# A time-mix and feed-forward kernel: the next block's normalisation moved to ScalarE, and weight splits spread over the first block's chunks

## The chip, the cores and the metric

The kernel runs on one core of a Trainium2 chip. The metric is the device time of one execution in microseconds (us); shorter is better. Five engines work side by side, each through its own instructions in order: TensorE (PE in the profile; its weight loads are PEld), VectorE (DVE), ScalarE (ACT), GpSimd (POOL) and SyncE (SP), which here only issues DMAs. An instruction that waits for another engine holds up everything behind it on its own engine.

## The reference

The input x is 4 x 1024 x 512. The kernel computes x + A(LN(x)) + F(LN(x)), where LN is a layer norm over the 512 features:

```python
xx = concat([x[:, 1:2], x[:, :-1]], axis=1) - x
k = (x + xx * mix_k) @ Wk.T          # 704 hidden
r = (x + xx * mix_r) @ Wr.T
state = state * w + relu(k_t)         # scan over time
out = layernorm((state * r) @ Wv.T) * gamma + beta      # A
D = gelu(float16(x) @ W0.T + bias0)   # 2048 hidden
E = float16(D) @ W1.T + bias1         # F
```

## The kernel before, in words

The tokens are cut into eight blocks of 512. Everything between the engines' instructions is written out by hand: the loops run under a manual schedule, so the order of the calls is the order on each engine.

**A block's loop.** Each block runs `for n in range(NN)` with NN = 16; one turn is called **chunk n** here. A chunk takes 128 of the 2048 hidden units. `up(i, n)` (L862) is the first product of the feed-forward part, eight matmuls of 512 columns into a PSUM bank `pd`: four with the high terms of W0 (`xf`, `w0h`), four with the low terms (`w0l`). The Gelu (L876, tile `d`, ScalarE) and a widening copy (L879) follow. `down` (L888) is the second product, eight matmuls with the low and then the high term of W1 (tile `w`). The up product runs two chunks ahead: in the first block, chunk n issues on TensorE up(n+2), then down(n), then a **piece** of the time-mix work, if the chunk has one. In the first block these are `raw_halves` (chunk 1), `three_pass` for r with h = 1 to 4 (chunks 3, 5, 7, 9; PSUM tiles `pa`, `pb`) and the output products `po` (chunks 12 to 15).

**Splits.** Weights and activations are split into terms so that fast matmuls keep the precision. `split` (L198) does it for W0 and W1: ScalarE writes the high term (L199), VectorE then the low one (L200). `split_kr` (begins L288) splits a tile of Wk or Wr: VectorE writes `wu` (L278) and `wd` (L285), ScalarE turns them into the first two terms `wt` (L294, L295), VectorE writes the third (L296); SyncE stores all three. `split_wv` (L308) does the same for Wv (`vu`, `vd`, `wv`); the half tile h = 5 takes two VectorE and four ScalarE instructions (L321, L322). All weights are split in the first block, a few at the start of the second, and reloaded later.

**What sets the order within a chunk.** First the followers of the chunk before (`after()` of a piece: ScalarE copies `a` out of `pa`, L707, VectorE makes `y`, L708, and so on), then the Gelu, then the jobs that `put(n, ...)` placed in `bg[n]`, in the order of the `put` calls, and last, in the first block, the split of W1 for chunk n+2: `waiting.append((d, load_w1(*nxt)))`. In the second block an odd chunk's Gelu comes after its jobs.

**PSUM.** `up`, the pieces and the output products take their banks in turn from one ring of four (`ps_mm`). A product can't start before the tile that had the bank four allocations earlier has been read by ScalarE or VectorE.

**The next block's x.** While the first block runs, the x of the second is loaded, its statistics are taken (`stats`, L354 and L355, VectorE), GpSimd makes 1/sqrt(var + eps) (`rstd_of`, L348 and L349), VectorE normalises (`norm_apply`, L358), then sixteen VectorE transposes (`turn`, L380) bring it into `xnT`. ScalarE makes the half-precision copy `x16` (L395) and the scaled copies (L403), VectorE mixes neighbouring tokens (L417, L421), ScalarE widens `x16` into `xf` (L442), which the second block's first up product reads.

Chunk by chunk, the first block's jobs that the change touches are: statistics in chunk 1, `norm_apply` in chunk 3, `first_kr(h)` (the split of Wr's tile h) in chunks 1, 3, 5, 7, transposes in chunks 4, 5, 7, 8, 9 (1, 4, 5, 1, 5 of them), `split_kr(1, 0, h)` for h = 2, 0, 1 in chunks 7, 10, 11, and `split_wv` for h = 0, 1, 2, 3, 5 in chunks 12, 13, 15, 15, 15; h = 4 follows in chunk 2 of the second block.

Of the kernel before, what the change touches and what calls it, by code (L numbers as in the profile page):

```python
# [14 lines left out]
AF = mybir.ActivationFunctionType  # L15
# [7 lines left out]
def time_mix_and_gelu_ffn(  # L23
# [32 lines left out]
    nc = tc.nc  # L56
# [4 lines left out]
    NS = TB // P  # L61
# [2 lines left out]
    Q = 32  # L64
    QS = 62
    RAW_OUT = 1
    WV_FIRST = {0: 12, 1: 13, 2: 15, 3: 15, 5: 15}
    S = 4096.0
    WS = 4096.0
    MASK = -4096  # L70
    OWN = dict(tag="q", bufs=QS)

    NF = HID // P
# [283 lines left out]
    def normalize(dst, src, mean, rstd):  # L357
        nc.vector.tensor_scalar(dst, src, mean, rstd, ALU.subtract, ALU.mult)  # L358

    norm = {}  # L360
# [9 lines left out]
    def norm_apply(i, xs):  # L370
        mv, rstd = norm.pop(i)
        for s in range(NS):
            normalize(xs[:, s, :], xs[:, s, :], mv[:, s, 0:1], rstd[:, s : s + 1])

    def transposed(xn, first=0, end=(P // Q) ** 2):
        src = xn.rearrange("p s (c i a) -> p s c i a", c=NC, a=Q)
# [531 lines left out]
    state = {}  # L908
# [53 lines left out]
    with tc.manual_schedule(engines=engines):  # L962
        for i in range(len(blocks)):
            j = i + 1
            tail = 4 if i == LAST else 0
            by_columns = range(NS // 2, NS) if tail else ()
            pieces, bg, early = defaultdict(list), defaultdict(list), defaultdict(list)

            def put(n, fn, *args, **home):
                bg[n].append(lambda: fn(*args, **home) if home else fn(*args))  # L970

            def first_kr(h):
                ks[0, 1, h] = split_kr(0, 1, h)
# [29 lines left out]
            if i == 0:  # L1003
                state["x"] = x_next
                piece(1, raw_halves, i)
                for h in range(1, NF):
                    piece(2 * h + 1, three_pass, i, 1, h)
                for c in range(NC):
                    put(2 + c - (c == 0), split_w0, 2, c)
                    put(c // 2, load_w0, 3, c)  # L1010
                    put(5 + c, split_w0, 3, c)
                put(1, stats, *range(NS))
                put(3, lambda: norm_apply(j, state["x"]))
                for c in range(NC):
                    put(c // 2, split_first_xr, c)
                for n, h in ((7, 2), (10, 0), (11, 1)):
                    put(n, split_kr, 1, 0, h, **OWN)
                for h in range(1, NF):
                    put(2 * h - 1, first_kr, h)
                put(4, turn, 0, 1)  # L1020
                put(5, turn, 1, 5)
                put(7, turn, 5, 10)
                put(8, turn, 10, 11)
                put(9, turn, 11, 16)
                put(9, load_late_constants)
                put(12, split_half)
                for g in range(NN // G):
                    put(11 + (g or NN // G), store_w0l, g)
                put(15, store_weights)
                mix_at = (11, 12, 13, 15)  # L1030
            else:
                order = [(0, h) for h in range(NF)] + [(1, h) for h in range(NF)]
                halves_ahead_of = (3 if i == LAST else NF, NF)
                for k, (kind, h) in enumerate(order):
                    for half in range(2):
                        if k == halves_ahead_of[half]:
                            piece(half_at[half], half_pass, i, half)
                    piece(full_at[k], three_pass, i, kind, h)
                    if (kind, h) not in made:
                        put({(0, 3): 1, (0, 4): 2, (1, 0): 4}[kind, h], fetch_kr, i, kind, h)  # L1040
                    elif k > 1:
                        put(full_at[k - 2], fetch_kr, i, kind, h)
                xr_at = {1: (2, 3, 4, 5), LAST: (1, 2, 2, 3)}.get(i, (2, 2, 3, 3))
                for c, n in enumerate(xr_at):
                    put(n, split_xr, i, c)
                if j <= LAST:
                    put(2, fetch_x)
                    for s in range(NS):
                        put(3 + s // 2 if i == 1 else 4, stats, s)
                    put(5, lambda: norm_apply(j, state["x"]))  # L1050
                    turns = (4, 4, 4, 4) if i == 1 else (4, 5, 4, 3)
                    for k in range(sum(turns)):
                        unit = next(n for n in range(4) if k < sum(turns[: n + 1]))
                        put(6 + unit, turn, k, k + 1)
                mix_at = (10, 12, 13, 14)
# [3 lines left out]
            if j <= LAST:  # L1059
                for c in range(NC):  # L1060
                    put((10, 10, 11, 12)[c], x16, j, c)
                for c, n in enumerate(mix_at):
                    early[n].append((j, c))
                    put(n, mixed, j, c)
                    put(n + (n == 10), split_xk, j, c)
                for h, n in {0: WV_FIRST, 1: {NF - 1: 2}}.get(i, {}).items():
                    put(n, split_wv, h)
                put(13, fetch_kr, j, 0, 0)
                put(14, fetch_kr, j, 0, 1)

            pe = [ps_e.tile([P, C], F32, tag="pe", name=f"pe_{i}_{s}") for s in range(NS)]
            for n in range(NN):
                ahead = n + AHEAD
                if ahead == NN and j <= LAST:
                    xf = next_xf
                nxt = (i, ahead) if ahead < NN else (j, ahead - NN)
                paired = i > 0 and n < NN - tail
                order = HIGH_FIRST if paired and n % 2 == 0 else LOW_FIRST
                end = lambda s: NN - tail if s in by_columns else NN
                products, gelu = up(*nxt) if nxt[0] <= LAST else (None, None)  # L1080

                def hidden(p):
                    if products:
                        products(p, order if paired else HIGH_FIRST)

                def outputs(p):
                    if n < NN - tail:
                        down(n, range(NS), *operands, p, order, end=end)

                if n < NN - tail:  # L1090
                    operands = waiting.pop(0)
                if not paired:
                    hidden(0)
                    hidden(1)
                elif n % 2 == 0:
                    hidden(0)
                else:
                    hidden(1)
                    outputs(1)
                    hidden(0)  # L1100
                works = [follow() for follow in followers]
                works = [w for w in works if next(w, works) is None]
                several(scaled_now, *early[n])
                if i == 0 or n == out_at[0] or (n > out_at[0] and i < RAW_OUT):
                    finished(*works)
                    works = []
                followers = []
                if behind_works:
                    waiting.append(behind_works.pop()())
                if gelu and not paired:  # L1110
                    d = gelu()
                if ahead + 1 == NN and j <= LAST:
                    next_xf = ffn_input(j)
                if not paired:
                    outputs(1)
                outputs(0)
                if gelu and i > 0:
                    w1 = load_w1(*nxt)
                    if not paired:
                        waiting.append((d, w1))  # L1120
                two_on = (i, ahead + 2) if ahead + 2 < NN else (j, ahead + 2 - NN)
                if two_on[0] <= LAST:
                    load_w0l(*two_on)
                jobs = [
                    lambda s=s: finish(i - 1, s, e16s[s])
                    for s in (2 * n, 2 * n + 1)
                    if s < len(e16s)
                ]
                for work, *args in pieces[n]:
                    followers.append(work(*args))  # L1130
                if i == 0 and ahead + 2 < NN:
                    load_w1_raw(ahead + 2)
                woven(works, jobs + bg[n])
                if i == 0:
                    waiting.append((d, load_w1(*nxt)))
                elif paired and n % 2 == 0:
                    hidden(1)
                    outputs(1)
                    behind_works.append(lambda gelu=gelu, w1=w1: (gelu(), w1))
                elif paired:  # L1140
                    waiting.append((gelu(), w1))
                store_weights()
# [66 lines left out]
```

## Time and profile before

| what | value |
|---|---|
| median of 3 runs | 858.14 us (857.48 to 858.91) |
| the profiled execution's own time | 857.93 us |
| its span | 856.1 us |
| TensorE | busy 847.0 us (99%), 3772 matmuls |
| VectorE | busy 687.1 us (80%), 1130 instructions |
| ScalarE | busy 438.1 us (51%), 748 instructions |
| GpSimd | busy 80.4 us (9%) |
| DMA | 166.72 MB, mean 195 GB/s |
| granted TensorE clock | 0.999 |

The first block lasts from the start to about 131 us, the second to about 234 us. A matmul is listed with the time that it takes to pass through, which overlaps its neighbours'; the distance from one start to the next is what it costs. For 512 columns that is 0.227 us, and 0.43 us for the unsplit products of the first block. In the timeline, equal instructions in a row are one line: start, time from first start to last end, engine, line, operation, tiles, count, and in square brackets the idle time before it with what ended it.

### The profile page before, as it was taken

What the parts mean: (1) busy time and instruction counts of PE and PEld (TensorE: products, weight loads), DVE (VectorE), ACT (ScalarE), POOL (GpSimd) and SP (SyncE); (2) the same over time, 40 slices, a digit from 0 to 9 for tenths busy, and PEclk for the clock granted to TensorE, in tenths of its full rate; (3) what the DMA queues carried; (4) which work ended last, traced back from release to release, by engine and by line L of the source; (5) the groups of instructions that cost most, each with busy time, mean ns of one, the idle gap of its engine ahead of it and who ended that gap; (6) DMA issues with size and microseconds to landing.
All of it is one profiled execution on the core that took longest, in us unless ns stands there. A gap on an engine that the chain in (4) does not pass through costs nothing.

```text
span 856.1 us, 11350 instructions
## 1 busy us (share of the span) xinstructions
PE 847.0 (99%) x3772; PEld 595.2 (70%) x3772; DVE 687.1 (80%) x1130; ACT 438.1 (51%) x748; POOL 80.4 (9%) x145
## 2 busy tenths in 40 slices
PE   9999999999999999999999999999999999999998
PEld 8556646667767767667777667677777667676776
DVE  6789898999868988789786897778796897876446
ACT  5857665546534563445725455344653545634422
POOL 1210000000211001000021001100011200200012
PEclk9999999999999999999999999999999999999999
DMA  9756995745467544856358455594465755467513
GB/s 279 252 178 239 306 282 193 249 151 182 148 230 225 172 136 149 288 165 209 130 170 284 148 180 172 159 308 146 151 193 161 272 173 181 127 220 247 169 54 111
DMA packets 120902, 166.72 MB, mean 195 GB/s; under 512 B 21487, under 2 KB 57740, under 8 KB 120844
## 3 DMA queue, kind: packets, MB, share of 16 engines
q1 hardware_dynamic: 120396, 165.34, 60.4%
q8 instruction: 30, 0.49, 0.2%
q10 hardware_dynamic: 448, 0.66, 0.2%
q14 instruction: 28, 0.23, 0.1%
HBM read 141.31 MB, written 24.64 MB: 194 GB/s over the span
## 4 chain that ended last, share of the span: by engine, by line
PE 82%; DVE 7%; DMA 5%; ACT 2%; issue 2%; SPq 2%; DVEq 0%; ACTq 0%
PE pd L862 22%; PE pe L888 22%; PE pa L695 14%; PE oa L792 7%; PE pb L446 7%; PE ob L800 4%; PE ph L724 3%; DMA x<-in_L_attn_x 2%; PE ob L802 1%; DMA krd<-wt 1%; DMA w0raw<-in_L_ffn_W 1%; SPq L239 1%; DVE w0l L200 1%; DVE wd L285 1%; ACT w L199 1%
## 5 line engine op out<-in xcount | busy, mean ns | idle before, releaser
L888 PE MATMUL pe<-w,d 128*128 128x512 f32 (+1 forms) x1008 | 262.9, 389 | 3.8 <-DVE w L200 3.4
L862 PE MATMUL pd<-xf,w0h 128*128 128x512 f32 x512 | 150.8, 415 | 0.1
L862 PE MATMUL pd<-x,w0l 128*128 128x512 f16 x512 | 132.2, 381 | 0.0
L876 ACT ACTIVATE d<-pd,late_sb 128x512 f16<-128x512 f32 x128 | 87.2, 681 | 75.4 <-PE pe L888 47.4
L862 PEld LDWEIGHTS pd<-xf,w0h 128*128 128x128 f32 x512 | 96.2, 188 | 28.4 <-issue 2.8
L888 PEld LDWEIGHTS pe<-w,d 128*128 128x128 f32 x504 | 94.7, 188 | 23.6 <-DVE e L835 1.2
L708 DVE SCALAR_TENSOR_TENSOR y<-pb,a 128x512 f32<-128x512 f32 x74 | 50.9, 688 | 65.5 <-PE pb L446 54.8
L888 PEld LDWEIGHTS <-d 128*128 128x128 f16 x524 | 50.6, 98 | 64.1 <-issue 5.1
L862 PEld LDWEIGHTS <-w0l 128*128 128x128 f16 x512 | 44.1, 98 | 62.2 <-issue 16.1
L879 ACT CAST d<-d 128x512 fp32r<-128x512 f16 x128 | 79.4, 620 | 10.3 <-PE pe L888 6.3
L380 DVE STREAM_TRANSPOSE xnT<-x 32x512 f32<-32x512 f32 x112 | 78.6, 702 | 2.2
L707 ACT ACTIVATE a<-pa 128x512 f32<-128x512 f32 x74 | 44.1, 596 | 70.2 <-PE pa L695 70.2
L348 POOL TENSOR_SCALAR ry<-mvy 128x1 f32<-128x1 f32 x32 | 18.9, 591 | 460.5 <-DVE mvy L355 460.5
L792 PE MATMUL oa<-wv,hg 128*128 128x512 f32 x140 | 54.5, 389 | 0.0
L792 PE MATMUL oa<-wv,lg 128*128 128x512 f32 x140 | 54.5, 389 | 0.0
L695 PE MATMUL pa<-lr,kr 128*128 128x512 f32 x136 | 52.9, 389 | 0.0
L695 PE MATMUL pa<-hr,kr 128*128 128x512 f32 x136 | 52.9, 389 | 0.0
L695 PE MATMUL pa<-hk,kr 128*128 128x512 f32 x132 | 51.4, 390 | 0.0
L695 PE MATMUL pa<-lk,kr 128*128 128x512 f32 x132 | 51.4, 389 | 0.0
L710 ACT ACTIVATE y<-y 128x512 f32<-128x512 f32 x35 | 22.1, 631 | 53.7 <-DVE y L708 53.7
L333 ACT CAST hg<-ug 128x512 fp32r<-128x512 f32 x35 | 21.7, 620 | 37.1 <-DVE ug L278 37.1
L807 DVE SCALAR_TENSOR_TENSOR oy<-ob,oa 128x512 f32<-128x512 f32 x28 | 19.3, 688 | 25.8 <-PE ob L802 25.8
(175 smaller groups left out, 1411.2 us busy)
## 6 DMA issues: line engine op xcount, KB each, us to landing
kr<-krd SPq DMA_DIRECT2D x201, 256.0 KB, 4.4
w<-w1d SPq DMA_DIRECT2D x112, 256.0 KB, 2.8
w<-w1d SPq DMA_DIRECT2D x112, 128.0 KB, 2.7
w0l<-w0d SPq DMA_DIRECT2D x108, 128.0 KB, 3.5
xres<-in_L_attn_x SPq DMA_DIRECT2D x32, 256.0 KB, 4.7
x<-in_L_attn_x SPq DMA_DIRECT2D x31, 256.0 KB, 5.0
krd<-wt SPq DMA_DIRECT2D x30, 256.0 KB, 3.3
out<-xres SPq DMA_DIRECT2D x28, 256.0 KB, 3.6
```

The costliest lines, as they stand in the source:

```text
L380: nc.vector.transpose(dst[i * Q : (i + 1) * Q, :, :, j, :], src[j * Q : (j + 1) * Q, :, :, i, :],)
L446: return nc.tensor.matmul(dst, w[:, c, :], src, start=(c == 0), stop=(c == NC - 1))
L695: nc.tensor.matmul(pa, w[p][:, c, :], xs[j, c][p], start=(c == 0 and p == 0), stop=(c == NC - 1 and p == 1),)
L707: nc.scalar.activation(a, pa, AF.Copy, scale=1.0 + 1.0 / S)
L708: nc.vector.scalar_tensor_tensor(y, pb, -1.0 / S, a, ALU.mult, ALU.add)
L724: nc.tensor.matmul(pa, w[:, c].rearrange("p two k -> p (two k)"), xs[j, c][p], start=(c == 0 and p == 0), stop=(c == NC - 1 and p == 1),)
L792: nc.tensor.matmul(pa, gs[i, h][p][:, cols], wv[h][p], start=(h == 0 and p == 0), stop=(h == NF - 1 and p == 1),)
L800: nc.tensor.matmul(pb, gs[i, h][2][:, cols], wv[h][2], start=(h == 0), stop=False)
L862: nc.tensor.matmul(pd, weights(c, p), src[c][p], start=(c == 0 and p == order[0]), stop=(c == NC - 1 and p == order[1]),)
L876: nc.scalar.activation(d16, pd, AF.Gelu, bias=b0_sb[:, n : n + 1], scale=1.0 / WS)
L879: nc.scalar.copy(d, d16)
L888: nc.tensor.matmul((sums or pe)[s], d[p][:, s * P : (s + 1) * P], w1[p][:, cols], start=(n == first and p == order[0]), stop=(n == end(s) ...
```

## The change

Six edits, all of them in what the first two blocks' chunks do:

1. The statistics of the second block's x move from chunk 1 to chunk 2.
2. Its normalisation leaves VectorE (one instruction for each of four tiles, chunk 3). ScalarE does it in two instructions a tile, one with the negated mean as bias and one with 1/std as scale, for two tiles in chunk 3 and two in chunk 4. GpSimd negates the means.
3. A new list, `behind_w1[n]`, is worked off after the chunk's split of W1. `first_kr`, `split_kr(1, 0, h)` and the ScalarE normalisation go there.
4. `split_kr(1, 0, 2)` moves from chunk 7 to chunk 4.
5. The transpose of chunk 4 joins those of chunk 5.
6. `split_wv` of the half tile h = 5 moves from chunk 15 of the first block to chunk 3 of the second, that of h = 4 from chunk 2 of the second to its chunk 6.

```diff
-    WV_FIRST = {0: 12, 1: 13, 2: 15, 3: 15, 5: 15}
+    WV_FIRST = {0: 12, 1: 13, 2: 15, 3: 15}
...
+    def norm_by_scalar(i, xs, tiles):
+        mv, rstd = norm[i]
+        if 0 in tiles:
+            nc.gpsimd.tensor_scalar_mul(mv[:, :, 0], mv[:, :, 0], -1.0)
+        for s in tiles:
+            for factors in ({"bias": mv[:, s, 0:1]}, {"scale": rstd[:, s : s + 1]}):
+                nc.scalar.activation(xs[:, s, :], xs[:, s, :], AF.Identity, **factors)
...
+            behind_w1 = defaultdict(list)
...
-                put(1, stats, *range(NS))
-                put(3, lambda: norm_apply(j, state["x"]))
+                put(2, stats, *range(NS))
+                behind_w1[3].append(lambda: norm_by_scalar(j, state["x"], range(2)))
+                behind_w1[4].append(lambda: norm_by_scalar(j, state["x"], range(2, NS)))
                 for c in range(NC):
                     put(c // 2, split_first_xr, c)
-                for n, h in ((7, 2), (10, 0), (11, 1)):
-                    put(n, split_kr, 1, 0, h, **OWN)
+                for n, h in ((4, 2), (10, 0), (11, 1)):
+                    behind_w1[n].append(lambda h=h: split_kr(1, 0, h, **OWN))
                 for h in range(1, NF):
-                    put(2 * h - 1, first_kr, h)
-                put(4, turn, 0, 1)
-                put(5, turn, 1, 5)
+                    behind_w1[2 * h - 1].append(lambda h=h: first_kr(h))
+                put(5, turn, 0, 5)
...
-                for h, n in {0: WV_FIRST, 1: {NF - 1: 2}}.get(i, {}).items():
+                for h, n in {0: WV_FIRST, 1: {NF: 3, NF - 1: 6}}.get(i, {}).items():
                     put(n, split_wv, h)
...
                     waiting.append((d, load_w1(*nxt)))
+                    for job in behind_w1[n]:
+                        job()
```

## The prediction

> **What bounds the kernel now.** I read the page first. Its chain of work that ended last is mostly TensorE, and the only sizeable wait in the groups of instructions is the second product's for VectorE's low term of W1:
>
> ```profile
> PE 82%; DVE 7%; DMA 5%; ACT 2%; issue 2%; SPq 2%; DVEq 0%; ACTq 0%
> L888 PE MATMUL pe<-w,d 128*128 128x512 f32 (+1 forms) x1008 | 262.9, 389 | 3.8 <-DVE w L200 3.4
> ```
>
> TensorE's timeline then says where: in the first block, at chunks 3, 5, 7 and 9.
>
> ```profile
> 52.16 1.95 PE L888 MATMUL pe<-w,d 128*128 128x512 f16 x8 [1.67 <-DVE w L200]
> 62.46 1.95 PE L888 MATMUL pe<-w,d 128*128 128x512 f16 x8 [0.26 <-DVE w L200]
> 73.05 1.94 PE L888 MATMUL pe<-w,d 128*128 128x512 f16 x8 [0.53 <-DVE w L200]
> 84.08 1.94 PE L888 MATMUL pe<-w,d 128*128 128x512 f16 x8 [0.99 <-DVE w L200]
> ```
>
> Between the starts of consecutive matmuls, less the usual 0.23, these four cost 1.81, 0.41, 0.68 and 1.14: 4.0 us. TensorE's other losses after 40 us come from the same starts: 1.3 us at 112 (the next block's `xf`), 1.3 at 132 (`e`, L835) and 0.7 at 154 (a bank that `a`, L707, must empty). From 156 us on it never waits. So what the change is worth is decided before 190 us, and any lateness of TensorE then stays to the end.
>
> **First block: statistics and W1 (edits 1 and 3).** Before, chunk 1 on VectorE goes: `w0l` (to 42.08), statistics 3.20, two splits of `xr` 3.77, `first_kr` 1.8 (three instructions 0.46, 0.72, 0.61 apart), then W1 of chunk 3, which lands at 52.10. Without statistics and `first_kr` ahead of it, that W1 starts at 42.08 + 3.77 = 45.85 and ends by 46.5; TensorE wants it at 50.35. The 1.81 goes; chunk 5's 0.41 goes too (its W1 by 57.4, wanted at 60.2). TensorE is then 2.2 us early. The statistics now start after chunk 2's half-tile work, at 52.4, and end at 55.6; W1 of chunk 4 follows at 55.6 to 56.2, wanted at 56.65: covered by 0.4 us.
>
> **ScalarE's normalisation (edits 2 and 4).** These rows price it:
>
> ```profile
> 57.52 1.91 DVE L358 TENSOR_SCALAR x<-x,mvx,rx 128x512 f32<-128x512 f32 x4
> 45.46 0.32 POOL L348 TENSOR_SCALAR rx<-mvx 128x4 f32<-128x4 f32 x1 [12.75 <-DVE mvx L355]
> 45.85 1.79 POOL L349 TENSOR_TENSOR rx<-rx,nhalf 128x4 f32<-128x4 f32 x1
> 168.20 1.04 POOL L349 TENSOR_TENSOR rx<-rx,nhalf 128x4 f32<-128x4 f32 x1
> 96.27 0.71 ACT L403 ACTIVATE xk<-xnT,rest_sb 128x512 f32<-128x512 f32 x1
> 96.89 0.71 ACT L403 ACTIVATE xr<-xnT,rest_sb 128x512 f32<-128x512 f32 x1
> 65.58 1.15 ACT L199 ACTIVATE w0h<-w0raw 128x512 fp32r<-128x512 f32 x2
> ```
>
> VectorE saves 1.83. The two-step form is not in the trace. Nearest is L403, which also takes a factor from a tile: 0.71 each, 0.62 apart; the second step needs the first, so 0.74 after it. Two tiles: 2.7 us, all four 5.4 (bounds: 8 x 0.48, the closest ScalarE spacing in this stage, = 3.9; 8 x 0.75 = 6.0). The negation on GpSimd is also unseen: 0.31, as its neighbour add (0.2 to 1.8).
>
> ScalarE reaches the normalisation at 54.0 and must wait. Statistics end 55.6, add and negation to 56.4, the power 1.79 more: 58.3. I take 1.79 and not 1.04 because it is the row of the same block, with VectorE busy beside it; the later five rows of 1.04 fall where VectorE waits for the result. With 1.04 all that follows is 0.8 earlier. [...]
>
> From 58.35, spaced as in the rows around 62 us, ScalarE issues: rest of two tiles 1.96, two `wt` 1.06, `a` 0.48, Gelu and cast 1.23, `w0h` 0.53, W1 0.53, two tiles 2.7, two `wt` of the split moved here from chunk 7 1.06, Gelu and cast 1.23, `w0h` 0.53 and the second `w0h`, 0.63. That is 11.95 us: the second `w0h` of chunk 5 is done at 70.3. Before it was done at 66.7. It is the last quarter of W0 for up(8), whose fourth matmul stood at 67.67 and, being 2.2 early, now wants it at 65.45. **So TensorE stalls 4.9 us in chunk 6 and is 2.7 late, where it had been 2.2 early.**
>
> [...]
>
> **To the end of the block (edits 3 and 5).** VectorE's transposes stand behind that `w0h`: `w0l` at 70.4, five transposes of 0.715 to 74.55, W1 of chunk 7 until 75.25, so TensorE starts at 75.3 against 73.05. Now `first_kr` follows W1, and the next chunk's `a` (L707) follows `first_kr` on ScalarE: `a` ends 2.2 after W1's term, the next piece wants its bank after 1.8. That adds 0.4: 2.7 late. The same in chunk 9: W1 at 86.4 (84.02), then 0.4: 2.8 late. W1 of chunks 10 to 12 is in time, the closest by 0.15.
>
> VectorE's own lateness grows: W1 of chunk 11 comes at 95.9 (91.06), that of 13 at 104.3 (102.19), and as the split of Wk's tile 1 now stands behind W1, chunk 14's at 113.6 (109.68). `xf` follows it on ScalarE: 115.9 against 112.00, so TensorE is 3.9 late. At 131 edit 6 takes 1.07 of VectorE ahead of `e` away; with TensorE later than VectorE by that, 1.1 of the 1.3 waited there comes back. **First block: 2.8 late.**
>
> SyncE issues the moved stores in the same new order: those of the tile-2 split stand ahead of W1's load for chunk 9, which is issued at about 69.5 instead of 66.27; ScalarE wants it at 81. Wv's loads go out at about 94.5 to 98 and are wanted from 102. I cost both at nothing; were the cover gone, they would cost 2 to 4 us.
>
> **Second block (edit 6).** VectorE, ScalarE and TensorE are all 2.8 late here, so I use the times of before and add that at the end. Without the tile-4 split in chunk 2, `a` runs at 152.0 and not 154.49, and TensorE's 0.7 at 154 goes. VectorE is 2.3 earlier: statistics 156.7 to 158.3. But then come the half tile's `vu` and `vd`, and its four ScalarE instructions stand in front of this Gelu:
>
> ```profile
> 158.12 0.68 ACT L876 ACTIVATE d<-pd,late_sb 128x512 f16<-128x512 f32 x1
> ```
>
> They run from 158.75 to 161.1 (they wait for `vd`, 159.45), so the Gelu ends at 161.8 instead of 158.8. It empties the bank that `three_pass` of k's tile 4 takes at 159.79: TensorE goes on 2.0 late. In chunk 6 the tile-4 split (1.8 on VectorE, behind transposes already 2.3 late) stands ahead of `a`, Gelu and `gh`. The Gelu of chunk 8 ends at 183.5 and the bank is wanted at 180.4: 3.15 late. The Gelu of chunk 9 ends at 187.5, wanted at 183.12: 4.4 late. **Second block: 4.4 late.** If the banks there have more room than I read, this is 0 or -0.7.
>
> **Sum.** 2.8 + 4.4 = 7.2 on the profiled execution's 857.93, which is 0.2 under the median of the runs: **865.0 us**.
>
> **Rivals.**
> - *It works as written*: W1's waits go and ScalarE's work hides. For it: ScalarE is busy only 51%, and idles 2.9 us before `wt` at 59.80. It decides where the second `w0h` is done by 65.45, 4.9 earlier than my sum. Price: -4.0, -0.7 at 154 and the 1.1 at `e`, 852 to 854 us. Chance 0.09.
> - *The moved Wv splits hide*: first block as above, second -0.7: 857.93 + 2.1 = 860.0. For it: VectorE still has 0.3 to 1 us idle in each 10 us there. Against: the waits are ScalarE's order, not VectorE's load. Chance 0.15.
> - *ScalarE is quick but the second block is not*: nothing lost in the first block, +3.7 in the second, 861.6. Needs the power early (0.8), a step at 0.48 (1.5) and a quicker restart. Chance 0.10.
> - *Two steps cost more, or stores hold SyncE*: the 6.0 and 2 to 4 us of loads: 868 to 872. Chance 0.13.
> - *About no change*, gains and losses even: 858. Chance 0.05.
> - The order as built shows all six edits on the engines, so that it doesn't do what it says is not a case.
>
> My forecast, 863 to 867.5, has 0.48. A measurement of this kernel can tell about 0.2% (1.7 us) from no change. The range of 859.5 to 869 takes in the middle two rivals and part of the fourth. Faster by over 0.2%: 0.09 and a little of the even case, 0.10; within: 0.07; slower: 0.83.
>
> **What the new profile would show.** Right: no wait for W1 at about 50 us; a gap on ScalarE before the new instructions, ended by GpSimd; TensorE waiting some 5 us in chunk 6 for `w0h` (L199); waits for the Gelu ahead of `pa` or `pb` in the second block. Wrong: up(8) without a wait, which would mean that ScalarE's steps are shorter or the statistics earlier; or no such waits after 155 us.

## The result, and the profile after

The changed kernel takes 868.5 us (median of 4 runs, 866.9 to 869.0) against 858.4 for the kernel before, measured beside it: ratio 1.0116, interval 1.0098 to 1.0133. The prediction was 865.0. The profiled execution takes 868.99 us (span 867.2) against 857.93.

On the page of the changed kernel, the chain of work that ended last gives ScalarE 4% instead of 2%, and in the groups of instructions the wait has changed its owner: the second product (L896) no longer waits, the first (L870) does.

```profile
PE 81%; DVE 7%; DMA 5%; ACT 4%; SPq 1%; issue 1%; POOL 0%; DVEq 0%; ACTq 0%
...
L896 PE MATMUL pe<-w,d 128*128 128x512 f32 (+1 forms) x1008 | 263.9, 391 | 0.1
L870 PE MATMUL pd<-xf,w0h 128*128 128x512 f32 x512 | 151.7, 418 | 7.1 <-ACT w0h L199 4.6
```

TensorE's timeline in chunks 3, 5 and 6 (start, us to the last end, engine, line, operation, and in brackets the idle time and what ended it):

```profile
51.01 1.95 PE L896 MATMUL pe<-w,d 128*128 128x512 f16 x8
60.89 1.95 PE L896 MATMUL pe<-w,d 128*128 128x512 f16 x8
71.06 0.79 PE L870 MATMUL pd<-xf,w0h 128*128 128x512 f32 x1 [4.65 <-ACT w0h L199]
71.66 1.93 PE L870 MATMUL pd<-x,w0l 128*128 128x512 f16 x4
73.38 2.38 PE L896 MATMUL pe<-w,d 128*128 128x512 f16 x8
```

The waits for W1 at 52 and 62 us are gone, and TensorE stands 4.65 us in chunk 6, waiting for the last quarter of W0. What the prediction didn't have is in the last two lines: four matmuls with the low terms take 1.93 us where they usually take 1.04, and eight of the second product 2.38 instead of 1.95. The table of windows (window, then its length, busy time and instructions of PE, PEld, DVE, ACT and POOL, then granted clock, DMA share, GB/s) says why:

```profile
66.00:80.00 14.00, 9.35 (x35) 5.18 (x34) 10.00 (x16) 8.94 (x17) 0.00 (x0) 0.88 0.52 181
116.00:132.00 16.00, 13.59 (x43) 6.52 (x36) 14.56 (x25) 9.06 (x16) 1.59 (x4) 0.79 0.99 275
72.00:74.00 2.00, 2.00 (x6) 0.76 (x5) 1.96 (x4) 0.00 (x0) 0.00 (x0) 0.50 0.44 167
```

The granted clock drops to 0.50 behind the wait, and again at 119 us behind a wait for `xf`. In the kernel before it is 1.00 in both stretches. The list of TensorE's waits (us in total, times, longest):

```profile
PE pd L870 <- ACT w0h L199: 4.6, 1, 4.6
PE pa L703 <- ACT d L884: 2.6, 2, 1.6
PE pd L870 <- ACT xf L450: 2.4, 1, 2.4
PE pb L454 <- ACT d L884: 0.8, 1, 0.8
```

ScalarE's timeline shows the two steps, and how they begin:

```profile
57.65 0.72 ACT L381 ACTIVATE x<-x,mvx 128x512 f32<-128x512 f32 x1 [2.80 <-POOL mvx L378]
59.07 0.73 ACT L381 ACTIVATE x<-x,rx 128x512 f32<-128x512 f32 x1 [0.70 <-POOL rx L349]
59.70 0.71 ACT L381 ACTIVATE x<-x,mvx 128x512 f32<-128x512 f32 x1
60.44 0.72 ACT L381 ACTIVATE x<-x,rx 128x512 f32<-128x512 f32 x1
...
69.87 1.14 ACT L199 ACTIVATE w0h<-w0raw 128x512 fp32r<-128x512 f32 x2
```

Both traces have 3772 matmuls in the same order, so each can be compared with itself. How much later TensorE starts the same matmul, by its time in the kernel before:

| at (before) | lag | what happened since the row above |
|---|---|---|
| 38.0 | +0.68 | the start, before any edit acts |
| 65.4 | -1.42 | two waits for W1 gone, -2.10 |
| 69.0 | +4.82 | wait for `w0h` 4.8, half clock 1.4 by here |
| 84.1 | +3.26 | W1's waits of chunks 7 and 9 gone, as TensorE is late itself |
| 111.6 | +3.86 | a bank for `a`, 0.6 |
| 113.2 | +6.35 | wait for `xf` |
| 121.1 | +8.66 | half clock behind it |
| 134.1 | +7.24 | the wait for `e` gone |
| 156.2 | +6.47 | the bank wait at 154 gone |
| 183.1 | +10.97 | waits in the second block |
| 850 | +11.06 | nothing more |

### The profile page after: what moved, and what is told of

Same layout as the page of the kernel before. It is cut to its first block, busy times and chain, and to the rows that moved or that the text cites. A ratio compares the mean times of both kernels' runs of the same rounds, so it can differ in the third digit from the quotient of the medians.

```text
span 867.2 us, 11355 instructions
## 1 busy us (share of the span) xinstructions
PE 851.9 (98%) x3772; PEld 598.2 (69%) x3772; DVE 685.8 (79%) x1126; ACT 442.6 (51%) x756; POOL 80.6 (9%) x146
## 4 chain that ended last, share of the span: by engine, by line
PE 81%; DVE 7%; DMA 5%; ACT 4%; SPq 1%; issue 1%; POOL 0%; DVEq 0%; ACTq 0%
PE pd L870 22%; PE pe L896 22%; PE pa L703 14%; PE oa L800 7%; PE pb L454 7%; PE ob L808 4%; PE ph L732 3%; DMA x<-in_L_attn_x 2%; PE ob L810 1%; DVE xnT L388 1%; PE po L759 1%; SPq L210 1%; DMA w1d<-w 1%; ACT d L884 1%; DMA w1raw<-in_L_ffn_W 1%
## 5 line engine op out<-in xcount | busy, mean ns | idle before, releaser
L896 PE MATMUL pe<-w,d 128*128 128x512 f32 (+1 forms) x1008 | 263.9, 391 | 0.1
L870 PE MATMUL pd<-xf,w0h 128*128 128x512 f32 x512 | 151.7, 418 | 7.1 <-ACT w0h L199 4.6
L870 PE MATMUL pd<-x,w0l 128*128 128x512 f16 x512 | 134.0, 385 | 0.0
L870 PEld LDWEIGHTS pd<-xf,w0h 128*128 128x128 f32 x512 | 96.7, 189 | 35.5 <-ACT w0h L199 5.3
L896 PEld LDWEIGHTS pe<-w,d 128*128 128x128 f32 x504 | 95.1, 189 | 22.9 <-ACT d L887 0.5
L896 PEld LDWEIGHTS <-d 128*128 128x128 f16 x524 | 51.0, 99 | 61.4 <-issue 3.1
L870 PEld LDWEIGHTS <-w0l 128*128 128x128 f16 x512 | 44.5, 99 | 63.1 <-issue 18.5
```

The costliest lines, as they stand in the source:

```text
L870: nc.tensor.matmul(pd, weights(c, p), src[c][p], start=(c == 0 and p == order[0]), stop=(c == NC - 1 and p == order[1]),)
L896: nc.tensor.matmul((sums or pe)[s], d[p][:, s * P : (s + 1) * P], w1[p][:, cols], start=(n == first and p == order[0]), stop=(n == end(s) ...
```

## The experiments

My theory after this comparison: three things cost, and each can be taken away alone. ScalarE's normalisation makes the stall at 66; waits of that length cost again through the clock; the moved splits of Wv hold Gelus in the second block. The rivals stand with each run. The runs were taken in five groups, each with the kernel before beside it, whose medians are 858.4 (the changed kernel), 857.9, 857.9, 858.5 and 857.8 in order. Runs of two groups are compared by what each is above its own.

**TensorE kept busy in the two waits.**

```diff
         def products(p, order=HIGH_FIRST):
+            if p == order[0]:
+                for _ in range({(0, 8): 20, (1, 0): 17}.get((i, n), 0)):
+                    nc.tensor.matmul(pd, weights(0, 1), src[0][1], start=True, stop=True)
```

> The changed kernel with 20 matmuls more ahead of the first block's up product 8 and 17 more ahead of the second block's up product 0; their sums are thrown away (each starts the bank anew), so the computation is the same. They fill the two long waits of TensorE (4.65 us at 66, 2.4 us at 116) with work that nothing waits for. Theory A: each of the two waits costs twice, once as a wait and once through the lowered granted clock behind it (0.50 from 71 to 74 us and from 119 to 125), about 1.3 and 2.4 us. Then the granted clock stays at 1.00 in both stretches, the eight matmuls of the down product behind up 8 take 1.8 us instead of 2.2, and the time falls by 2.0 to 3.7, to 864.8 to 866.5. Rival B: the matmuls there are slow for another reason (their operands come late, or ScalarE and VectorE use the same memory), and extra matmuls only sit in the way: 868 to 869, with the same slow stretches.

Measured 867.85 us (1.0114, 1.0099 to 1.0129). The windows of this run:

```profile
66.00:80.00 14.00, 13.46 (x59) 7.63 (x58) 10.08 (x16) 8.94 (x17) 0.00 (x0) 1.00 0.53 178
116.00:132.00 16.00, 15.98 (x64) 8.28 (x61) 14.27 (x24) 11.10 (x20) 1.59 (x4) 1.00 0.94 261
```

The mechanism of theory A holds, B falls: the clock stays at 1.00, and from 113 to 121 the lag no longer grows (6.92 to 6.64, instead of 6.35 to 8.66). But the whole gains little: 867.85 is 0.6 us under the changed kernel's median, and 9.95 above its own kernel before, where the changed kernel is 10.1 above; A's least was 2.0. TensorE is 2.0 us earlier at 131 than in the changed kernel, and the second block takes 1.3 of that back: the Gelus come when ScalarE and VectorE reach them. There TensorE waits 2.90 us at 165 instead of 1.60, and runs at 0.65 from 167.6 to 170. An earlier TensorE waits longer: TensorE isn't what this kernel's first two blocks hang on.

**Edit 6 taken back, and edit 6 alone.**

```diff
-    WV_FIRST = {0: 12, 1: 13, 2: 15, 3: 15}
+    WV_FIRST = {0: 12, 1: 13, 2: 15, 3: 15, 5: 15}
...
-                for h, n in {0: WV_FIRST, 1: {NF: 3, NF - 1: 6}}.get(i, {}).items():
+                for h, n in {0: WV_FIRST, 1: {NF - 1: 2}}.get(i, {}).items():
```

> The changed kernel without edit 6: the splits of Wv's half tile and tile 4 stand where they stood before. Theory A (as in the prediction): the waits at 166, 179, 189 and 193 us come from these splits' instructions ahead of the Gelu on ScalarE; they go (-4.6), the bank wait at 154 comes back (+0.7) and up to 1.1 us of the wait for e at the end of the first block: 864.6 to 865.7. Rival B: they come from the lateness that the first block hands on to VectorE and ScalarE, whatever is split there: the waits stay and the time is 867 to 869.

> The kernel before with edit 6 alone. Theory A: about 1.1 us of the wait for e at 131 us goes, the bank wait at 154 goes (-0.7), and the waits behind the moved splits come (+4.6): 860.5 to 861.5, with gaps of about 2 us and 1 to 3 us in chunks 4, 8 and 9 of the second block. Rival B: those waits need the lateness of the changed first block, and here the splits hide: 856 to 857.

Without edit 6: 863.4 us (1.0064, 1.0047 to 1.0081), 5.5 above the kernel before, so 4.6 better than with it; the four waits are gone, and the lag stays between 5.1 and 5.4 from 134 us on. Alone on the kernel before: 861.3 us (1.0038, 1.0023 to 1.0053). Theory A holds in both; the first time is 1.2 us under its bounds. Alone, the lag falls from -0.28 to -1.43 at `e`, to -2.16 at 154, and then rises to 3.39. The largest piece, on TensorE's timeline:

```profile
160.69 0.50 PE L695 MATMUL pa<-hk,wt 128*128 128x512 f32 x1 [2.90 <-ACT d L876]
```

So edit 6 gains 1.9 us, pays 5.5, and needs nothing of the rest of the change to do so.

**The last quarter of W0 a chunk earlier.**

```diff
-                    put(2 + c - (c == 0), split_w0, 2, c)
+                    put(min(4, 2 + c - (c == 0)), split_w0, 2, c)
```

> The changed kernel with the split of the last quarter of W0 for up product 8 taken one chunk earlier, ahead of the second normalisation pair, so that ScalarE's order and not its amount of work changes. Theory A: the wait for w0h and the low clock behind it are then gone at 66 us, but VectorE (its transposes wait for the normalisation, and after 72 us it is nearly always busy) still sets when xf comes, 116 to 118 us, and TensorE waits there instead: 865.5 to 867.5. Rival B (as the sum of the prediction had it): TensorE's wait at 66 is what the rest of the block inherits, so all of 4.65 plus 1.3 comes back: 862 to 863.

866.85 us (1.0103, 1.0088 to 1.0119), 1.1 us better than the changed kernel: theory A's number, but another place. Up product 8 no longer waits for `w0h`, and TensorE stands 4.04 us at the next W1. Its timeline, then VectorE's:

```profile
75.08 3.57 PE L896 MATMUL pe<-w,d 128*128 128x512 f16 x8 [4.04 <-DVE w L200]
```

```profile
70.14 0.69 DVE L200 SCALAR_TENSOR_TENSOR w0l<-w0raw,w0h 128x512 f16<-128x512 f32 x1 [2.75 <-ACT w0h L199]
70.75 3.55 DVE L388 STREAM_TRANSPOSE xnT<-x 32x512 f32<-32x512 f32 x5
74.33 0.69 DVE L200 SCALAR_TENSOR_TENSOR w<-w1raw,w 128x512 f16<-128x512 f32 x1
```

VectorE idles 2.75 us for ScalarE, then does its transposes, then W1. The 4.65 us wait that I had made the centre of the first block was one face of VectorE's lateness; with it gone, TensorE waits one chunk later.

**The normalisation back on VectorE, and in one step on ScalarE** (both without edit 6, so against 863.4).

```diff
-        if 0 in tiles:
-            nc.gpsimd.tensor_scalar_mul(mv[:, :, 0], mv[:, :, 0], -1.0)
...
-            for factors in ({"bias": mv[:, s, 0:1]}, {"scale": rstd[:, s : s + 1]}):
-                nc.scalar.activation(xs[:, s, :], xs[:, s, :], AF.Identity, **factors)
+            normalize(xs[:, s, :], xs[:, s, :], mv[:, s, 0:1], rstd[:, s : s + 1])
```

```diff
             nc.gpsimd.tensor_scalar_mul(mv[:, :, 0], mv[:, :, 0], -1.0)
+            nc.gpsimd.tensor_tensor(mv[:, :, 0], mv[:, :, 0], rstd, ALU.mult)
...
+            factors = {"bias": mv[:, s, 0:1], "scale": rstd[:, s : s + 1]}
+            nc.scalar.activation(xs[:, s, :], xs[:, s, :], AF.Identity, **factors)
```

> The changed kernel without edit 6, and with the normalisation in one instruction a tile on VectorE again, at the places where ScalarE had it (behind W1's split in chunks 3 and 4, in chunk 3 behind first_kr). The rest of edits 1, 3, 4 and 5 stays. To be held against the changed kernel without edit 6, 863.4. Theory A: ScalarE's eight instructions made the wait for w0h at 66 us and VectorE's 2.9 us of idle beside it, so both go, the granted clock stays at 1.00, and W1's waits at 52 and 62 us stay away; but VectorE's load still sets when xf comes (112 to 113.5 us), so TensorE's lead of some 2 us is lost there again: 857 to 859. Rival B: the new order of statistics, first_kr and the tile-2 split is itself too late for the transposes: over 860. Rival C: the lead is kept to the end: 855 to 856.

> The changed kernel without edit 6, and with ScalarE's normalisation in one instruction a tile instead of two (scale 1/std, bias minus mean times 1/std, which one more GpSimd instruction makes). Against 863.4. Theory A: the amount of work in front of w0h counts: 4 x 0.68 = 2.7 us less, so the wait at 66 falls from 4.65 to about 2.0, short enough that the granted clock stays at 1.00 there, and xf comes 2 to 3 earlier: 859.5 to 861.5. Rival B: what counts is when GpSimd's power comes and the place in the order: the wait at 66 stays over 3.5 us and the time is 862.5 to 863.5.

On VectorE: 859.95 us (1.0023, 1.0014 to 1.0033), 3.5 better, against A's 857 to 859 and just under B's 860. ScalarE's normalisation is thus worth 3.5 us of the loss, and the order that is left (edits 1, 3, 4, 5) about 2.1. With the 4.6 of edit 6 (3.4 when it stands alone) that is the changed kernel's 10.1. The trace with the normalisation on VectorE:

```profile
66.51 0.50 PE L867 MATMUL pd<-xf,w0h 128*128 128x512 f32 x1 [1.24 <-ACT w0h L199]
...
114.51 2.07 PE L867 MATMUL pd<-xf,w0h 128*128 128x512 f32 x4 [2.48 <-ACT xf L447]
```

The wait for `w0h` didn't go, it shrank to 1.24. TensorE is still 0.64 us early at 111 and has lost that and 1.8 more by 115, waiting for `xf`; the half clock behind it (0.57 from 116.5 to 120.5) takes another 1.6. In one step: 862.0 us (1.0045, 1.0030 to 1.0060), between A and B. The wait shrank from 4.65 to 3.35, not to 2.0: the first pair can't start before GpSimd has both factors (58.85 instead of 57.65), so only the second pair's saving of 1.3 us counts; and the clock fell all the same (0.51 from 69 to 71).

**Only first_kr and the statistics behind W1; then `xf` first as well.**

```diff
-                put(1, stats, *range(NS))
...
-                    put(2 * h - 1, first_kr, h)
+                    behind_w1[2 * h - 1].append(lambda h=h: first_kr(h))
+                behind_w1[1].append(lambda: stats(*range(NS)))
...
+                    for job in behind_w1[n]:
+                        job()
```

```diff
+                if ahead + 1 == NN and j <= LAST and i == 0:
+                    next_xf = ffn_input(j)
                 several(scaled_now, *early[n])
...
-                if ahead + 1 == NN and j <= LAST:
+                if ahead + 1 == NN and j <= LAST and i > 0:
```

> The kernel before, with first_kr behind W1's split (as in edit 3) and the statistics behind it too, in chunk 1. The normalisation, transposes, tile-2 split and Wv's splits are as before. Theory A: W1's four waits (4.0 us) go almost wholly, and TensorE is 3 to 4 us early at 110, but xf (112.0 us) and e (131 us) are set by VectorE's and ScalarE's order and don't move, so TensorE waits there: 857 to 858.5. Rival B: TensorE's waits for W1 were what the time hung on (the change's own idea): 854 to 855.5.

> As the run before this one (first_kr and statistics behind W1's split), and xf made ahead of the scaled copies and the Gelu in its chunk on ScalarE: xf begins at about 109.6 instead of 112.0. Theory A (ScalarE's order at xf held back the lead): 1.2 to 2.4 us better than that run, with what is left waiting for e at 131: 855 to 857. Rival B: the lead is lost at e anyhow, so that nothing is gained over that run: within 0.5 of it.

860.4 us (1.0027, 1.0018 to 1.0037) and 863.6 us (1.0061, 1.0046 to 1.0076): slower than all four forecasts. In the first, TensorE is 2.5 us early at 67 and has nothing left at 86: W1 of chunk 9 comes at 83.57 where it came at 84.08, so TensorE only waits longer (2.49 instead of 0.99). VectorE's sum of work ahead of that W1 is the same. With `first_kr` behind W1, VectorE then waits 0.46 us for ScalarE's `a` and 0.35 for its `w0h`, and W1 of chunk 11 is late too (TensorE waits 1.59). With `xf` first, `xf` isn't waited for at all, but ScalarE's four copies stand ahead of the scaled copies that VectorE mixes. VectorE's timeline shows the wait, and where `e` then stands:

```profile
114.83 0.75 DVE L417 SCALAR_TENSOR_TENSOR xk<-xnT,mix_sb,xk 128x512 f32<-128x512 f32 x1 [2.00 <-ACT xk L403]
...
135.22 2.48 DVE L835 SCALAR_TENSOR_TENSOR e<-pe,b_sb 128x512 f16<-128x512 f32 x4
```

TensorE waits 3.22 us there, with the clock at 0.50 from 138 to 140. `e` begins on VectorE at 131.0 in the kernel before, at 133.3 with the first of these edits, at 135.2 with both. By the time at which VectorE reaches `e`, the kernels without edit 6 stand nearly in the order of their times: 131.0 (857.9), 132.8 (859.95, VectorE's normalisation), 133.3 (860.4), 134.9 (862.0, one step), 135.2 (863.6), 136.2 (863.4). **The theory that I kept: from about 57 us VectorE's row of work sets the end of the first block.** What it idles there, waiting for ScalarE, the kernel loses; what TensorE idles it mostly doesn't. The traces bear it out. VectorE comes to `e` straight from other work, without a wait for TensorE, and behind `e` (at 134 us of the kernel before) TensorE is as late as VectorE's `e` is, within 0.03 us, in ten of the twelve runs of this section; in the other two, the normalisation on VectorE and `xf` first, it is 0.3 and 0.4 later. The changed kernel itself is the exception: its `e` is 5.1 us late and TensorE 7.2, because of the half clock behind `xf`. With TensorE kept busy both are 5.5 late, and the end comes 0.7 us earlier in the traces: the second block holds TensorE either way.

**Three tries at a better kernel on that theory.** One-step normalisation on ScalarE in chunk 3, where it idles 2.9 us; the Wv splits of the second block behind the Gelu; both.

```diff
+        nc.gpsimd.tensor_scalar_mul(mv[:, :, 0], mv[:, :, 0], -1.0)
+        nc.gpsimd.tensor_tensor(mv[:, :, 0], mv[:, :, 0], rstd, ALU.mult)
+        for s in range(NS):
+            factors = {"bias": mv[:, s, 0:1], "scale": rstd[:, s : s + 1]}
+            nc.scalar.activation(xs[:, s, :], xs[:, s, :], AF.Identity, **factors)
...
-                put(3, lambda: norm_apply(j, state["x"]))
+                put(3, lambda: norm_by_scalar(j, state["x"]))
```

```diff
-    WV_FIRST = {0: 12, 1: 13, 2: 15, 3: 15, 5: 15}
+    WV_FIRST = {0: 12, 1: 13, 2: 15, 3: 15}
...
-                for h, n in {0: WV_FIRST, 1: {NF - 1: 2}}.get(i, {}).items():
+                for h, n in {0: WV_FIRST}.get(i, {}).items():
...
                 elif paired:
                     waiting.append((gelu(), w1))
+                    if i == 1 and n in (3, 5):
+                        split_wv({3: NF, 5: NF - 1}[n])
```

> The kernel before with one thing changed: the normalisation in chunk 3 is done by ScalarE in one instruction a tile (GpSimd makes the bias, minus mean times 1/std), at the place where VectorE had it. The statistics stay in chunk 1, so that GpSimd's power is long done (47.6 us), and ScalarE has 2.9 us without work there, from 56.9 to 59.8. Theory A: VectorE's row of work sets the first block from 57 us on, so taking 1.83 us off it pulls W1 of chunks 5, 7 and 9, xf and e forward, while ScalarE's 2.5 us fill an idle stretch: 1 to 2 us faster, 856.0 to 857.0; the changed kernel lost by the place and time of the move, not by the move. Rival B: a normalisation on ScalarE costs more than VectorE saves wherever it stands: 858.5 to 860.

> The kernel before with edit 6 in another place: the half tile of Wv is split in chunk 3 of the second block, tile 4 in chunk 5, both behind that chunk's Gelu instead of ahead of it. Against the kernel before with edit 6 as in the change (861.3). Theory A: what cost 4.8 us there is that ScalarE's split instructions wait for VectorE's in front of a Gelu that empties a bank; behind the Gelu ScalarE has idle time, so only the gains are left (about 1.2 at e, 0.7 at 154): 855.8 to 856.8. Rival B: the splits' work on VectorE and ScalarE in the second block is what costs, whatever the order: 859 to 861.

> Both of the two runs before this one together. Theory A: their gains lie at different places and add, but for the part at e that both claim: 854.5 to 855.5. Rival B: TensorE's earliness from the first is lost at xf or e, so that it is no better than the better one of the two (within 0.4 us).

The first: 857.6 us (0.9995, 0.9986 to 1.0004), no difference that can be told, between A and B. VectorE's timeline, then ScalarE's:

```profile
61.13 0.69 DVE L200 SCALAR_TENSOR_TENSOR w<-w1raw,w 128x512 f16<-128x512 f32 x1 [1.91 <-ACT w L199]
```

```profile
56.61 2.92 ACT L381 ACTIVATE x<-x,mvx,rx 128x512 f32<-128x512 f32 x4
```

VectorE saved 1.83 and then idled 1.91, because W1's high term stands behind the four instructions on ScalarE. The second, the moved splits: 860.5 us (1.0035, 1.0025 to 1.0045), theory A wrong. The wait of 2.90 at 160 has become 1.02, but the tile-4 split's 1.8 us on VectorE delay the chain of the half piece (`ph`, `gh`), the Gelu behind it and so TensorE at 183:

```profile
160.72 1.19 PE L446 MATMUL pb<-mk,wt 128*128 128x512 f32 x4 [1.02 <-ACT a L707]
...
185.44 0.50 PE L695 MATMUL pa<-hr,kr 128*128 128x512 f32 x1 [1.87 <-ACT d L876]
```

Behind the Gelu the splits cost TensorE 4.5 us in the second block, ahead of it 5.5. VectorE is busy 5.4 to 5.9 of every 6 us from 158 to 206 us in the kernel before, so neither place has room for them. Both together: 862.1 us (1.0047, 1.0032 to 1.0062), worse than either. TensorE is as late at 183 us as in the second run (2.4 and 2.3 behind the kernel before), but then the clock falls to 0.50 from 186.5 to 190.0, and it is 4.1 late behind that.

The last run takes VectorE's lost 1.91 away:

```diff
-                put(3, lambda: norm_apply(j, state["x"]))
...
+                put(1, lambda: norm_by_scalar(j, state["x"], range(2)))
+                put(3, lambda: norm_by_scalar(j, state["x"], range(2, NS)))
...
-                put(4, turn, 0, 1)
-                put(5, turn, 1, 5)
+                put(5, turn, 2, 5)
...
+                    if n == 3:
+                        turn(0, 2)
```

> The kernel before, with the normalisation on ScalarE in one instruction a tile, two tiles in chunk 1 (ScalarE waits 1.2 us for VectorE at 48.3, and GpSimd's factors are there by 48.3) and two in chunk 3 (idle from 56.6), and with two of the sixteen transposes moved from chunks 4 and 5 to behind W1's split in chunk 3, where VectorE would wait for TensorE's sum (about 60.2 to 61.5 us). In the last run with ScalarE's normalisation VectorE lost what it had saved (1.83) to a wait of 1.91 for W1's high term behind the four instructions. Theory A: VectorE's row sets the first block from 57 us on; here it keeps 1.5 to 1.8 us of the saving, so W1's waits at 62, 73 and 84 shrink, and xf and e come 1.5 us earlier: 855.8 to 857.2. Rival B: ScalarE's later order (a, Gelu, w0h, the 1.1 us waits for stores of W1) takes it back again: 857.5 to 859.

857.06 us against 857.78 (0.9994, 0.9985 to 1.0003). VectorE's W1 of chunk 5 waits 0.49 instead of 1.91, and `e` begins at 129.9 instead of 131.0, a gain of 1.1 of the 1.83. TensorE's trace agrees: of the four waits for W1 the two at 62 and 73 us are gone, and it is 0.2 us early at 38, 1.4 at 84 and 1.1 behind `e` and at the end. So 0.9 us of the gain lasts in the profiled execution, on the path that the theory names. The median is inside A's bounds, but the interval includes no change, so a kernel faster than the one before isn't shown.

## Why the prediction was right or wrong

The direction and the three costs (ScalarE's normalisation, the order behind W1, the moved splits) were right. On the profiled executions it said +7.2 and +11.06 came: 868.5 is past the forecast of 863 to 867.5 and near the end of the range of 859.5 to 869. Point by point, by its own steps:

- **Statistics and W1.** Right: both waits gone, TensorE 2.1 us earlier by 65 us (2.2 forecast).
- **ScalarE's normalisation.** Right: steps 0.63 and 0.74 apart, four instructions 2.7 us. GpSimd's power took 1.45, between 1.04 and 1.79; the negation took 0.5, not 0.31. VectorE was busy for 1.42 of those 1.45 us; in the kernel before it was busy for 1.66 of the 1.79, and for 0.68 of the 1.04 at 168. What slows the power, no run shows. And of the 5.4 forecast against VectorE's 1.83, a good part was the second step: in one step the four tiles take ScalarE 2.92 us against VectorE's 1.91. The second `w0h` was done at 71.0, as forecast (70.3), when the 0.7 us are taken off by which all of this run is later from the start.
- **The stall of 4.9 us in chunk 6.** Right in size (4.8 above a usual start) and cause. The half clock behind it, which had no price, cost 1.4 more, but not for long: at 84 us the changed kernel and the run with TensorE kept busy are equally late, 2.58 us when what each had at 38 us is taken off. Its role was wrong. I took it as TensorE's loss that the rest inherits; the run with W0 earlier took it away and gained 1.1 us, so most of it was VectorE's lateness, seen at one place.
- **Chunks 7 to 9.** 2.8 late forecast; 3.86 less the 0.68 of the start is 3.2.
- **`xf`, 3.9 late.** This is the step that failed. `xf` began at 118.28 instead of 112.00, 6.3 late. Less 0.7 of the start, that is 1.7 more than forecast. What I cost at nothing, the stores in SyncE's new order, is in the trace: ScalarE's W1 waited 1.10 us for the store that empties its buffer, a wait that the kernel before doesn't have, and VectorE waited behind it,

```profile
106.03 0.63 ACT L199 ACTIVATE w<-w1raw 128x512 fp32r<-128x512 f32 x1 [1.10 <-DMA w1d<-w]
```

```profile
106.69 0.69 DVE L200 SCALAR_TENSOR_TENSOR w<-w1raw,w 128x512 f16<-128x512 f32 x1 [1.20 <-ACT w L199]
```

  and the half clock behind `xf` added 2.3, which the run with TensorE kept busy took away. That the stores cause most of the 1.7 is read from the trace; no run took them away, so it stays open.
- **`e` gives back 1.1.** It gave 1.4.
- **Second block, 4.4 late.** 3.8 (7.24 to 11.06), at the places named: Gelus of chunks 5, 8 and 9 (2.0, 1.2, 1.4 us between starts). The run with edit 6 alone shows the mechanism by itself. The rival that the splits hide is out.
- **The sum.** The 3.9 us that it missed: start 0.7, first block 3.8 (1.8 up to `xf`, 2.3 in the half clock behind it, less 0.3 more given back at `e`), less 0.6 in the second block. The start's 0.7 is there before any edit acts; other runs' lags at 38 us are between -0.3 and +0.4.

The half clock had no price in the forecast: the stall of 4.9 us was counted as a wait alone. The kernel before gave no case to price it by: from 4.88 to 854.80 us its clock is 1.00, and its longest wait there is 1.67. The changed kernel gave two: 0.50 for 3.4 us behind the wait of 4.65, and 0.50 for 6.8 us behind the wait of 2.41 for `xf`.

## What to carry to other kernels

When an engine is relieved, ask whose order it then waits in: here VectorE gave away 1.83 us of work and idled as long for ScalarE, and the tensor engine's waits, which the page shows first, were only where VectorE's lateness became visible. To find the engine that sets a stretch, take one wait away and see whether the time follows or the wait moves. Price a forecast stall of some us twice, once as a wait and once for the slower matmuls behind it (here 1.4 us behind the wait of 4.65, 2.3 behind that of 2.41), and ask then whether TensorE sets the end there: in this kernel, full clock in both stretches was worth 0.1 to 0.6 us of the whole.

## What the runs showed of the hardware

In these traces the clock changes on a grid. The trace's clock record has its edges in the changed kernel at 70.83, 74.25, 118.62 and 125.45 us: 3.41, 44.37 and 6.83 apart, which is 1, 13 and 2 times 3.413. All six changes of that record, from 9.39 to 866.14, lie on the same grid. In the run with W0 earlier three edges are at 73.64, 80.47 and 165.80: 2 and 25 times 3.413 apart. The kernel before changes its clock at 4.88 and at 854.80, 249 times apart. What makes the grid, no run shows. Two waits of 2.90 us for the same Gelu fall on it differently; first with edit 6 alone, then with TensorE kept busy (columns as above, by stretches of the grid):

```profile
155.50:158.91 3.41, 2.28 (x11) 1.55 (x9) 2.38 (x6) 1.51 (x3) 0.00 (x0) 1.00 0.36 119
158.91:162.32 3.41, 1.64 (x7) 1.38 (x8) 0.51 (x1) 2.80 (x5) 0.00 (x0) 1.00 0.87 248
162.33:165.73 3.40, 3.40 (x18) 1.78 (x17) 3.33 (x6) 1.70 (x3) 0.00 (x0) 1.00 0.70 264
```

```profile
164.89:168.30 3.41, 0.68 (x3) 0.59 (x4) 0.03 (x1) 3.27 (x6) 0.00 (x0) 1.00 0.57 163
168.31:171.71 3.40, 3.40 (x10) 2.62 (x9) 2.89 (x5) 2.10 (x4) 0.00 (x0) 0.50 0.70 252
```

The first wait is cut in two by an edge, and no stretch has TensorE idle for more than 1.77 us; the clock stays at 1.00. The second lies almost wholly in one stretch, idle for 2.73, and the next is at 0.50. Other stretches just ahead of a half clock had TensorE idle for 3.41 and 2.08 us in the changed kernel, 3.40 and 2.10 without edit 6, 3.29 and 2.00 in one step, 2.59 with W0 earlier; but also for 1.86 with `xf` first, and for 1.19 with the normalisation on VectorE, where the four matmuls behind the wait took 2.07 us (1.08 in most rows of that run). The wait of 2.49 us for W1 at 83 left the clock at 1.00 in both runs that have it, and with `xf` first 1.90 of it fell into one stretch, so idle time as the profile counts it isn't all that decides. Nor is it known what brings the full clock back: in the changed kernel it stayed at 0.50 for a second stretch, from 122.03, though TensorE was idle for only 0.33 us of the first.
